# A second fixed order for the mixer: outputs in halves, the next unit's decays ahead, tokens normalized a unit earlier

## The chip, the cores and the metric

The kernel runs on one core of a Trainium2 chip. The metric is the device time of one execution in microseconds (us), and a version is judged by the median of several. The engines are called by the names of the profile: PE (matmuls and transposes), DVE (vector), ACT (scalar, with its function tables), POOL (GpSimd) and SP (issues the DMAs). Everything is float32.

## The reference

The input is 8 images of 32 x 32 positions with 128 channels, treated as 8 batches of T = 1024 tokens with C = 128 channels.

```python
x = x + conv_attention(group_norm(x))            # 4 heads of 32, q and k with unit length
t = to_tokens(x)
t = t + mamba(layer_norm(t), fwd) + reverse(mamba(reverse(layer_norm(t)), bwd))
t = t + stu(layer_norm(t))                       # spectral filters, by FFT
```

The change lies in the second line, the mixer, and at the end of attention. For one batch and one direction:

```python
z, xbc, dt = split(x @ in_proj)                  # 256, 256 + 64 + 64, 4
xh, Bm, Cm = split(silu(causal_conv(xbc, 4)))    # 4 heads of 64; state size 64
dt = softplus(dt + dt_bias); dA = dt * -exp(A_log)
# in 16 chunks of 64 tokens:
Y_diag = C B^T * L * (x dt)                      # L = exp(segment sums of dA), inside a chunk
states = B^T (decay_to_end * x dt)               # one state a chunk
new    = state + carry * chunk_decay             # passed on from chunk to chunk
Y_off  = C carry * decay_from_start
y  = (Y_diag + Y_off + D x) * silu(z)
out = rms_norm(y) @ out_proj
```

## The kernel before

Four stages follow each other. The **setup** loads X, normalizes it, makes q, k and v, and begins the tables of the last stage. **Attention** runs over 128 units (batch b, half of the queries, block j of 128 keys), one in 2.75 us; eight units make one half of a batch. The **mixer** runs over 16 units (batch b, direction d). The **last stage** (layer norm, filters by transforms, sum) begins when the last sum of the mixer has been stored.

*Order.* Work that the text leaves to the framework's scheduler is placed by it. Within `manual_schedule(engines=IN_ORDER)` PE, DVE, ACT and POOL issue exactly in the order of the text. Attention and the mixer's loop stand in such a region; the preparation of the mixer's first unit (from `normalize(0, ...)` to `activate_bc(first)`) does not.

*Attention.* In step n, `scores` computes score products `pt` (L486) on PE into a pool of three buffers, and ACT takes their exponential `pr` (L491). `weigh` multiplies `pr` of step n - 1 with v on PE (`po`, L506) and adds pairs of `pr` on DVE (`two`, L515); `total` sums these over keys with a matmul (`pd`, L526). At the end of a half, `project` takes the reciprocal of the denominators in pieces over the following steps, keeps their extremes in `most` and `least`, multiplies (`av`, L546), projects on PE (`py`, L550) and adds onto X (L554).

Meanwhile POOL mixes the filter weights of the last stage (`mixed`, L231 and L233, and `both`, L245). That text stands ahead of attention's, in the setup. Each part comes by a DMA on SP's queue and is scaled and added.

*Mixer.* The inputs of a unit are made during the unit before it. `normalize` takes mean and variance of a batch's tokens (`b_st`, `b_mv`, DVE) and, through `rsqrt`, the factor `ln_r` on POOL (L117, L119); `normalized` makes `b_shift` (DVE, L651) and the tokens `b_x` (ACT, eight instructions, L654). `turn_tokens` transposes them (`px`) and copies them to `bxt`. `steps` makes the step sizes (`pd`, L685, then small DVE operations and two ACT operations) and `da`. `spread` makes `dau`, 128 x 2048, on POOL (L717). `project_x` and `convolve` make `xs` (projection `pp` on PE, copy `xp` on ACT, three DVE operations for each half, L756), `project_z` the gate `zs`, `project_bc` and `activate_bc` `bt` and `ct`.

In the unit itself, in this order:
- `decays`: three small matmuls into the PSUM tile `misc` (L801), and their exponentials `rest` (L803) and `dec` (L807) on ACT.
- `turn_x`: transposes of `xs` (`sx`, L817) and the product `xdt` (DVE, L820, twice).
- `turn_sums` of the unit before: two transposes in the same `misc` (L1022), `rms_v` (DVE, L1024), `rms` (POOL, L1026).
- `turn_b`: `sb` (PE, L834), its halves go to `bk` (ACT, L842) and `gm` (DVE, L854).
- `decayed_x`: `xdd` (DVE, L849, twice), then `gm`.
- `add_up` of the unit before: eight sums from `spo` onto X (DVE, L1033); with d = 1 X is then stored.
- `between`: `pl` (PE, L863), `lm` = exponential (ACT, L870).
- `chunk_states` and `pass_states`: `pst` (PE, L900), then the chain of states on DVE (L914, L917, 29 instructions), half of which a DMA moves to the other partitions (`moved`).
- `from_start`: `pe` (PE, L880), `ec` = exponential (ACT, L887).
- `weigh_decays`: `lm` times `gm` (L938, twice) and `ec` times `ct` (L942, twice, 128 x 1024 each) on DVE.
- `outputs`: 240 small matmuls `sy` (L966) for all 16 chunks, into two PSUM tiles.
- `gate`: `y` (DVE, L981, L989) and its squares `sq` (ACT, L990).
- `project_out`: `spo` (PE, L996); `square_sums`: `misc` (L1008) and the copy `sums` (ACT, L1016).

The wide PSUM tiles come in two pools of two buffers each: `ps_w` (`px`, `pd`, `pp`, `pz`, `pb`, `sx`, `sb`, `pl`, `pe`) and `ps_s` (`misc`, `pst`, `sy`, `spo`). `bxt`, `dau` and the tokens have one buffer each.

Of the kernel before, what the change touches and what calls it, by code (L numbers as in the profile page):

```python
# [44 lines left out]
def fast_kernel(ctx: ExitStack, tc: tile.TileContext, a: dict, out: bass.AP, bad: bass.AP):  # L45
# [7 lines left out]
    tables_pool = middle.enter_context(tc.tile_pool(name="tables_pool", bufs=1, side="right"))  # L53
    early = ctx.enter_context(ExitStack())
# [3 lines left out]
    def ctile(shape, name):  # L58
        pool = const if name in LASTING else tables_pool if name in ("fwd", "m_u") else passing
        return pool.tile(shape, F32, tag=name, name=name)  # L60
# [314 lines left out]

    with ExitStack() as s:
        keepq = s.enter_context(tc.tile_pool(name="a_q", bufs=1))
        qs, ks, vs = [], [], []  # L380
        with ExitStack() as s2:
# [79 lines left out]
            load_ssm_weights(p1)  # L461

        p1 = s.enter_context(tc.tile_pool(name="a_1", bufs=1))
# [5 lines left out]


        most = p1.tile([P, 2 * B], F32, name="most")
        least = p1.tile([P, 2 * B], F32, name="least")
# [61 lines left out]
        def project(b, half, av, pd):  # L534

            den = p1.tile([P, 512], F32, tag="den", name=f"den{b}_{half}")
            nc.vector.tensor_copy(den, pd)
            yield
            for i in range(4):
                cols = slice(i * P, (i + 1) * P)  # L540
                nc.vector.reciprocal(den[:, cols], den[:, cols])
                if i % 2:
                    yield
            nc.vector.tensor_reduce(most[:, 2 * b + half : 2 * b + half + 1], den, AX.X, ALU.max)
            nc.vector.tensor_reduce(least[:, 2 * b + half : 2 * b + half + 1], den, AX.X, ALU.min)
            nc.vector.tensor_tensor(av, av, den, ALU.mult)  # L546
            yield
            py = ps_t.tile([P, 4, C], F32, tag="t", name=f"py{b}_{half}")
            for i in range(4):
                nc.tensor.matmul(  # L550
                    py[:, i, :], lhsT=av[:, i * P : (i + 1) * P], rhs=wout, start=True, stop=True
                )
            to = X[b][:, half * 4 : half * 4 + 4, :]
            nc.vector.tensor_tensor(to, to, py, ALU.add)  # L554
# [4 lines left out]
        for n in range(len(units) + 2):  # L559
            if n < len(units):  # L560
                prs[n] = scores(*units[n])
            if 2 <= n and units[n - 2][2] % 2:
                b, half, j = units[n - 2]
                total(b, half)
                if j == NT - 1:
                    ending = project(b, half, sums.pop("av"), sums["d"])
            if 1 <= n < len(units) + 1:
                b, half, j = units[n - 1]
                weigh(b, half, j, prs.pop(n - 1))
                if j == NT - 1:  # L570
                    av = p1.tile([P, 512], F32, tag="av", name=f"av{b}_{half}")
                    nc.vector.tensor_copy(av, sums["o"])
                    sums["av"] = av
            next(ending, None)
        for _ in ending:
            pass


        far = ctile([P, 4], "far")
        nc.vector.tensor_reduce(far[:, 0:1], most, AX.X, ALU.max)  # L580
        nc.vector.tensor_reduce(far[:, 1:2], least, AX.X, ALU.min)
        nc.vector.tensor_scalar(far[:, 2:3], far[:, 0:1], 1e25, None, ALU.is_gt)
        nc.vector.tensor_scalar(far[:, 3:4], far[:, 1:2], 1e-30, None, ALU.is_lt)
        pf = ps_o.tile([1, 2], F32, tag="d", name="pf")
        nc.tensor.matmul(pf, lhsT=ones[:, 0:1], rhs=far[:, 2:4], start=True, stop=True)
        nc.vector.tensor_reduce(far[0:1, 0:1], pf, AX.X, ALU.add)
        nc.vector.tensor_copy(bad, far[0:1, 0:1])

    def layer_norm(pool, b, name):
        st = pool.tile([P, NT, 6], F32, tag="ln_st", name=f"{name}_st{b}")  # L590
        mv = pool.tile([P, NT, 2], F32, tag="ln_mv", name=f"{name}_mv{b}")
        for j in range(NT):
            nc.vector.bn_stats(st[:, j, :], X[b][:, j, :])
        for j in range(NT):
            nc.vector.bn_aggr(mv[:, j, :], st[:, j, :])
        rstd = rsqrt(pool, mv[:, :, 1], NT, 1.0, 1e-5, "ln_r")
        xn = pool.tile([P, NT, C], F32, tag="ln_x", name=f"{name}_x{b}")
        for j in range(NT):
            nc.vector.tensor_scalar(
                xn[:, j, :], X[b][:, j, :], mv[:, j, 0:1], rstd[:, j : j + 1], ALU.subtract, ALU.mult  # L600
            )
        return xn
# [7 lines left out]
    with ExitStack() as s:  # L610
# [27 lines left out]
        def normalize(b, seq):  # L638
            st = p1.tile([P, NT, 6], F32, tag="ln_st", name=f"b_st{b}")
            mv = p1.tile([P, NT, 2], F32, tag="ln_mv", name=f"b_mv{b}")  # L640
            for j in range(NT):
                nc.vector.bn_stats(st[:, j, :], X[b][:, j, :])
            for j in range(NT):
                nc.vector.bn_aggr(mv[:, j, :], st[:, j, :])
            rstd = rsqrt(p1, mv[:, :, 1], NT, 1.0, 1e-5, "ln_r")
            seq["mv"], seq["rstd"] = mv, rstd

        def normalized(b, seq):
            mv, rstd = seq["mv"], seq["rstd"]
            shift = p1.tile([P, NT], F32, tag="ln_s", name=f"b_shift{b}")  # L650
            nc.vector.scalar_tensor_tensor(shift, mv[:, :, 0], -1.0, rstd, ALU.mult, ALU.mult)  # L651
            xn = p1.tile([P, NT, C], F32, tag="ln_x", name=f"b_x{b}")
            for j in range(NT):
                nc.scalar.activation(  # L654
                    xn[:, j, :], X[b][:, j, :], AF.Identity, bias=shift[:, j : j + 1], scale=rstd[:, j : j + 1]
                )
            seq["xn"] = xn

        def turn_tokens(b, seq):
            xn = seq["xn"]  # L660
# [3 lines left out]
            xt = p1.tile([P, T + 2 * pad], F32, tag="xt", name=f"bxt{b}")  # L664
# [5 lines left out]
        def steps(b, seq):  # L670
# [27 lines left out]
            yield  # L698
            u = small("sp_u")
            nc.vector.tensor_scalar(u, e, 1.0, None, ALU.add)  # L700
            lg = small("sp_l")
# [11 lines left out]
        def spread(u):  # L713

            u.dt, u.da = u.seq["dt"][:, :, u.heads], u.seq["da"][:, :, u.heads]
            u.dau = p1.tile([P, NT, NH, L], F32, tag="dau", name=f"dau{u.tag}")
# [46 lines left out]
        def project_z(u):  # L763
            u.zs = p2.tile([P, 2, T], F32, tag="zs", name=f"zs{u.tag}")
            for n in range(2):
                pz = projected(u, slice(n * P, (n + 1) * P), f"pz{u.tag}_{n}")
                nc.scalar.activation(u.zs[:, n, :], pz, AF.Silu)  # L767
# [29 lines left out]
        def decays(u, misc):  # L797

            pd = misc[:, 768 : 768 + 3 * NT * NH].rearrange("p (i j h) -> p i j h", i=3, j=NT)
# [45 lines left out]
        def decayed_x(u):  # L845
            u.xdd = p1.tile([P, NT, NH, HP], F32, tag="xdd", name=f"xdd{u.tag}")
            for i in range(2):
# [3 lines left out]
                )  # L851

            u.gm = p1.tile([P, NT, L], F32, tag="gm", name=f"gm{u.tag}")
            nc.vector.tensor_tensor(u.gm, u.pg, upto[u.d].unsqueeze(1).to_broadcast([P, NT, L]), ALU.mult)  # L854
# [80 lines left out]
        def weigh_decays(u):  # L935
            for i in range(2):
                js = slice(4 * i, 4 * i + 4)
                nc.vector.tensor_tensor(  # L938
                    u.lm[:, js], u.lm[:, js], u.gm[:, js].unsqueeze(2).to_broadcast([P, 4, NH, L]), ALU.mult
                )  # L940
            for r in range(2):
                nc.vector.tensor_tensor(  # L942
                    u.ec[:, r], u.ec[:, r], u.ct.unsqueeze(2).to_broadcast([P, NT, 2, L]), ALU.mult
                )

        def outputs(u):

            u.py = [
                wide_psum(ps_s, f"sy{u.tag}_{c}").rearrange("p (n j l) -> p n j l", n=2, j=NT) for c in range(2)
            ]  # L950
            before = {at: k for k, at in enumerate(u.chunks[1:])}
            for j in range(NT) if u.d == 0 else reversed(range(NT)):
# [92 lines left out]
        normalize(0, seqs[0])  # L1045
        normalized(0, seqs[0])
        turn_tokens(0, seqs[0])
        for _ in steps(0, seqs[0]):
            pass
        first = units[0]  # L1050
        spread(first)
        project_x(first)
        project_z(first)
        project_bc(first)
        for n in range(2):
            convolve(first, n)
            activate_x(first, n)
        activate_bc(first)

        s.enter_context(tc.manual_schedule(engines=IN_ORDER))  # L1060
        last = None
        misc = wide_psum(ps_s, "misc")
        for at, u in enumerate(units):
            following = units[at + 1] if at + 1 < len(units) else None
            fresh = following and following.d == 0
            decays(u, misc)
            turn_x(u)
            if last:
                turn_sums(last, misc)
            turn_b(u)  # L1070
            decayed_x(u)
            if last:
                add_up(last)
            if fresh:
                turn_tokens(following.b, following.seq)
            between(u)
            going = iter(())
            if fresh:
                going = steps(following.b, following.seq)
                next(going)  # L1080
            chunk_states(u)
            pass_states(u)
            from_start(u)
            next(going, None)
            if following:
                project_x(following)
                next(going, None)
                spread(following)
                project_z(following)
            weigh_decays(u)  # L1090
            outputs(u)
            if following:
                convolve(following, 0)
                activate_x(following, 0)
                project_bc(following)
# [6 lines left out]
            if u.d == 0 and u.b + 1 < B:  # L1102
                normalize(u.b + 1, seqs[u.b + 1])
# [3 lines left out]
            if u.d == 0 and u.b + 1 < B:  # L1107
                normalized(u.b + 1, seqs[u.b + 1])
# [1080 lines left out]
```

## Time and profile before

| | us |
|---|---|
| median of 3 runs | 1711.31 |
| lowest, highest | 1708.39, 1714.41 |
| the profiled execution's own time | 1705.17 |
| its span in the profile | 1703.5 |
| attention | about 130 to 478.7 |
| first unit's preparation, to its first state | 478.7 to 530.67 |
| mixer from its first state to its end | 530.67 to 1241 |
| last stage | 1241 to the end |
| mean granted clock of PE | 0.949 |

| engine | busy us of the span | share |
|---|---|---|
| PE | 1497.4 | 88% |
| DVE | 1181.0 | 69% |
| ACT | 874.4 | 51% |
| POOL | 446.4 | 26% |

The shares are means over stages that differ, so the stages are read one by one. Lines such as L938 are those of the kernel before. In a group of instructions, "out<-in" gives the program's names; "idle before, <-releaser" is the time that the engine stood just before them and what ended it. A "stretch" is a part of the span with the busy time of each engine in it.

### The profile page before, as it was taken

Reading aid. Unit: us, or ns where it says so; the run is one execution under the profiler, and the core shown is the slowest. Engines: PE = TensorE matmul, PEld = TensorE weight load, DVE = VectorE, ACT = ScalarE, POOL = GpSimd, SP = SyncE. Lnnn points to the kernel's source line nnn. Section 1 sums busy time; section 2 is a strip of 40 time slices with the busy share of each in tenths; the row PEclk is TensorE's granted clock in tenths of the full one; section 3 lists DMA queues with packets and bytes.
Section 4 is the critical chain, followed back from the end, with each engine's and each line's share of the span. In section 5 each row is a group of like instructions: output and inputs, shape, how many; then the busy total and the mean of one; then the engine's idle time right before and its main releaser. Section 6 shows DMA issues by size and latency. Waiting matters only on the chain. (4 is left out here: it accounts for less than half of the span.)

```text
span 1703.5 us, 45615 instructions
## 1 busy us (share of the span) xinstructions
PE 1497.4 (88%) x20118; PEld 926.3 (54%) x20118; DVE 1181.0 (69%) x2211; ACT 874.4 (51%) x1198; POOL 446.4 (26%) x504
## 2 busy tenths in 40 slices
PE   4679999999979898988888889989757999999977
PEld 3432333332335565565555555555546888888862
DVE  6757778777756787877777787778544366677644
ACT  2337776677746555454555555555253255555530
POOL 6428999300010212112111111111045410100100
PEclk9899999999979899999999999989878999999998
DMA  5001212000000000000000000000046722322238
GB/s 143 0 11 55 59 60 63 22 2 1 1 1 13 13 26 13 26 11 23 7 25 13 13 26 13 26 13 26 13 149 211 199 60 60 79 67 72 69 93 315
DMA packets 131958, 89.03 MB, mean 52 GB/s; under 512 B 41480, under 2 KB 114824, under 8 KB 131752
## 3 DMA queue, kind: packets, MB, share of 16 engines
q1 hardware_dynamic: 129640, 81.84, 17.1%
q8 instruction: 160, 2.62, 0.7%
q10 hardware_dynamic: 2112, 4.19, 0.6%
q14 instruction: 46, 0.38, 0.1%
HBM read 44.60 MB, written 33.55 MB: 46 GB/s over the span
## 5 line engine op out<-in xcount | busy, mean ns | idle before, releaser
L491 ACT ACTIVATE pr<-pt 128x1024 f32<-128x1024 f32 x256 | 248.1, 1021 | 101.8 <-PE pt L486 96.9
L1268 DVE COPY gs<-pg 128x512 f32<-128x512 f32 x256 | 164.8, 686 | 84.4 <-PE pg L1257 79.6
L1270 ACT COPY gs<-pg 128x512 f32<-128x512 f32 x256 | 138.8, 595 | 145.9 <-PE pg L1257 130.3
L515 DVE TENSOR_TENSOR two<-pr,pr 128x1024 f32<-128x1024 f32 x128 | 158.3, 1277 | 28.0 <-PE pd L526 28.0
L486 PE MATMUL pt<-q,k 32*128 32x512 f32 x1024 | 162.8, 643 | 4.8 <-DVE taps L362 3.5
L1257 PE MATMUL pg<-taps,mst 32*128 32x128 f32 x4096 | 160.3, 287 | 6.5 <-ACT gs L1270 6.5
L1257 PEld LDWEIGHTS pg<-taps,mst 32*128 32x128 f32 x4096 | 135.9, 189 | 31.3 <-issue 16.7
L1291 PE MATMUL py<-gs,u 128*32 128x128 f32 (+1 forms) x4096 | 144.8, 282 | 0.4 <-ACT gs L1270 0.4
L506 PE MATMUL po<-pr,v 128*32 128x512 f32 x1024 | 136.7, 602 | 0.0
L756 DVE SCALAR_TENSOR_TENSOR xs<-xp,cw,xs 128x1024 f32<-128x1024 f32 x96 | 123.9, 1293 | 4.6 <-ACT xs L748 2.4
L1291 PEld LDWEIGHTS py<-gs,u 128*32 128x32 f32 (+1 forms) x4096 | 112.5, 143 | 15.5 <-ACT gs L1270 0.6
L717 POOL TENSOR_TENSOR dau<-upto,da 128x2048 f32<-128x2048 f32 x16 | 63.8, 3989 | 202.3 <-DVE da L709 125.6
L776 PE MATMUL pb<-bxt,wbc 128*128 128x512 f32 x256 | 114.2, 598 | 0.7 <-ACT zs L767 0.7
L1026 POOL TENSOR_TENSOR rms<-rms_v,mhalf 128x8 f32<-128x8 f32 x16 | 39.3, 2457 | 279.3 <-DVE rms_v L1024 279.3
L486 PEld LDWEIGHTS pt<-q,k 32*128 32x128 f32 x1024 | 55.3, 184 | 102.9 <-PE pt L486 40.2
L966 PE MATMUL sy<-lm,xdt 64*64 64x64 f32 x2048 | 81.7, 247 | 22.2 <-DVE lm L938 19.7
L966 PEld LDWEIGHTS sy<-lm,xdt 64*64 64x64 f32 x2048 | 74.8, 155 | 36.9 <-DVE lm L938 20.6
L1280 POOL TENSOR_SCALAR u<-u 128x512 f32<-128x512 f32 x16 | 23.8, 1490 | 248.0 <-DMA u<-ud 248.0
L917 DVE SCALAR_TENSOR_TENSOR state<-state,dec,pst 128x64 f32<-128x64 f32 x448 | 87.3, 275 | 1.1
L776 PEld LDWEIGHTS pb<-bxt,wbc 128*128 128x128 f32 x256 | 47.2, 189 | 55.6 <-issue 53.8
L966 PE MATMUL sy<-ec,state 64*64 64x64 f32 x960 | 64.2, 245 | 14.0 <-DVE ec L942 11.3
L506 PEld LDWEIGHTS po<-pr,v 128*32 128x32 f32 x1024 | 27.3, 109 | 87.7 <-issue 87.4
(278 smaller groups left out, 2938.5 us busy)
## 6 DMA issues: line engine op xcount, KB each, us to landing
ud<-sp SPq DMA_DIRECT2D x8, 1024.0 KB
u<-ud SPq DMA_DIRECT2D x32, 256.0 KB
yd<-sums SPq DMA_DIRECT2D x32, 256.0 KB
moved<-state SPq DMA_DIRECT2D x48, 128.0 KB
yt<-yd SPq DMA_DIRECT2D x6, 1024.0 KB
X<-in_x SPq DMA_DIRECT2D x8, 512.0 KB
part_p<-in_L_ffn_M_phi_plus SPq DMA_DIRECT2D x32, 128.0 KB
part_m<-in_L_ffn_M_phi_minus SPq DMA_DIRECT2D x32, 128.0 KB
```

Of the source, the lines that this page charges most:

```text
L486: nc.tensor.matmul(pt[:, i, :], lhsT=k[rows, j * P : (j + 1) * P], rhs=q[rows, cols], start=True, stop=True)
L491: nc.scalar.activation(pr[:, 2 * g : 2 * g + 2, :].rearrange("p i t -> p (i t)"), pt.rearrange("p i t -> p (i t)"), AF.Exp,)
L506: nc.tensor.matmul(po[rows, :], lhsT=vs[b][:, j, rows], rhs=pr[:, h, :], start=(j == 0), stop=(j == NT - 1))
L515: nc.vector.tensor_tensor(two, sums["pr"][:, 2 * g : 2 * g + 2, :], pr[:, 2 * g : 2 * g + 2, :], ALU.add)
L756: nc.vector.scalar_tensor_tensor(acc, xp[:, at : at + T], cw[u.d][:, n, i : i + 1], acc, ALU.mult, ALU.add)
L776: nc.tensor.matmul(u.pb[:, i * 512 : (i + 1) * 512], lhsT=wbc[u.d][:, k, :], rhs=xt[:, at : at + 512], start=(k == 0), stop=(k == KC - 1),)
L917: nc.vector.scalar_tensor_tensor(u.state[:, k, h, :], u.state[:, k - 1, h, :], u.dec[:, c, j, h : h + 1], u.pst[c][:, j, h, :], ALU.mult, ...
L966: nc.tensor.matmul(u.py[c][h * HP : (h + 1) * HP, r, j, :], lhsT=left, rhs=right, start=(kind == 0), stop=(kind == 1 or k is None),)
L1257: nc.tensor.matmul(pts[g][:, e, :], lhsT=mst[rows, n * 4 + e, :], rhs=taps[rows, cols].rearrange("p f q m i -> p (f q m i)"), start=True, ...
L1268: nc.vector.tensor_copy(to, frm)
L1270: nc.scalar.copy(to, frm)
L1291: nc.tensor.matmul(py[t * 32 : t * 32 + 32 - 16 * m, q, :], lhsT=u[:, i, m:, :, :, q * FC + f].rearrange("p k b i -> p (k b i)"), rhs=mats ...
```

## The change

All of it is order, buffers and the split of two operations; what is computed stays the same, and the number of PE instructions changes by one.

1. **The mixer's loop.** `turn_x` and `turn_sums` of the unit before now stand ahead of `decays`; the decays use other columns of `misc`. `gm` moves between the two halves of `xdd`. `turn_tokens` of the next batch and `between` stand ahead of `add_up`. `spread` of the next unit stands right behind `chunk_states`, ahead of the chain of states, instead of behind `project_x`. `dau` and `bxt` get two buffers.
2. **Outputs in halves.** `weigh_decays` and `outputs` run in two halves of eight chunks, in the direction of the unit: half 0, its outputs, then half 1. `ec` times `ct` thus becomes four instructions of 128 x 512 for two of 128 x 1024. `project_z` is split: its first half stands ahead of the first outputs, its second behind `convolve` of half 0.
3. **Tokens a unit earlier.** A batch is turned, and its steps are made, in the unit with d = 0 of the batch before, instead of in its unit with d = 1; its normalization begins one unit before that, and `normalized` follows in the unit with d = 1.
4. **The first unit.** Its preparation is written out in the order by hand, behind attention. Batch 0 is normalized inside attention: `normalize(bridge, 0)` at step n = 40 and `normalized(0, ...)` at n = 44 (both halves of X[0] are done by step 22). The projection of the last half of attention, the comparison of the denominators and the normalization of batch 1 stand behind the first unit's preparation.
5. **Memory.** A pool `bridge` holds `av`, `most`, `least` and the normalized tokens over both stages; some constants move to a pool that is closed before attention.

The core of the diff:

```diff
@@ attention
-        def project(b, half, av, pd):
+        def weighted(b, half, av, pd):
...
+            if (b, half) != (B - 1, 1):
+                project(b, half, av, ps_t.tile([P, 4, C], F32, tag="t", name=f"py{b}_{half}"))
...
             next(ending, None)
+            if n == 40:
+                early_norm = normalize(bridge, 0)
+            if n == 44:
+                xns[0] = normalized(0, bridge, *early_norm)
@@ parts of the mixer
-            xt = p1.tile([P, T + 2 * pad], F32, tag="xt", name=f"bxt{b}")
+            xt = p2.tile([P, T + 2 * pad], F32, tag="xt", name=f"bxt{b}")
...
-            u.dau = p1.tile([P, NT, NH, L], F32, tag="dau", name=f"dau{u.tag}")
+            u.dau = p2.tile([P, NT, NH, L], F32, tag="dau", name=f"dau{u.tag}")
...
-            pd = misc[:, 768 : 768 + 3 * NT * NH].rearrange("p (i j h) -> p i j h", i=3, j=NT)
+            pd = misc[:, 256 : 256 + 3 * NT * NH].rearrange("p (i j h) -> p i j h", i=3, j=NT)
...
-        def weigh_decays(u):
-            for i in range(2):
-                js = slice(4 * i, 4 * i + 4)
-                nc.vector.tensor_tensor(
-                    u.lm[:, js], u.lm[:, js], u.gm[:, js].unsqueeze(2).to_broadcast([P, 4, NH, L]), ALU.mult
-                )
+        def weigh_decays(u, half):
+
+            i = half ^ u.d
+            js = slice(4 * i, 4 * i + 4)
+            nc.vector.tensor_tensor(
+                u.lm[:, js], u.lm[:, js], u.gm[:, js].unsqueeze(2).to_broadcast([P, 4, NH, L]), ALU.mult
+            )
             for r in range(2):
                 nc.vector.tensor_tensor(
-                    u.ec[:, r], u.ec[:, r], u.ct.unsqueeze(2).to_broadcast([P, NT, 2, L]), ALU.mult
-                )
+                    u.ec[:, r, js], u.ec[:, r, js], u.ct[:, js].unsqueeze(2).to_broadcast([P, 4, 2, L]), ALU.mult
+                )
@@ the first unit, and the loop
-        normalize(0, seqs[0])
-        normalized(0, seqs[0])
-        turn_tokens(0, seqs[0])
...
+        s.enter_context(tc.manual_schedule(engines=IN_ORDER))
+        first, norms = units[0], {}
+        turn_tokens(0, seqs[0])
+        project_x(first)
+        going = steps(0, seqs[0])
+        next(going)
+        project_z(first, 0)
+        next(going)
+        next(going, None)
+        spread(first)
+        convolve(first, 0)
+        project_z(first, 1)
+        project_bc(first)
+        activate_x(first, 0)
+        convolve(first, 1)
+        activate_bc(first)
+        activate_x(first, 1)
+        project(B - 1, 1, av, wide_psum(ps_w, "last_py")[:, :512].rearrange("p (i c) -> p i c", i=4))
+        compare_denominators(most, least, wide_psum(ps_w, "pf")[0:1, :2])
+        xns[1] = normalized(1, bridge, *normalize(bridge, 1))
...
-            fresh = following and following.d == 0
-            decays(u, misc)
+
+            going, fresh = iter(()), u.b + 1 if u.d == 0 and u.b + 1 < B else 0
             turn_x(u)
             if last:
                 turn_sums(last, misc)
+            decays(u, misc)
             turn_b(u)
             decayed_x(u)
+            if fresh:
+                turn_tokens(fresh, seqs[fresh])
+            between(u)
             if last:
                 add_up(last)
             if fresh:
-                turn_tokens(following.b, following.seq)
-            between(u)
-            going = iter(())
-            if fresh:
-                going = steps(following.b, following.seq)
+                going = steps(fresh, seqs[fresh])
                 next(going)
+            if u.d == 1 and u.b + 2 < B:
+                xns[u.b + 2] = normalized(u.b + 2, bridge, *norms.pop(u.b + 2))
             chunk_states(u)
+            if following:
+                spread(following)
             pass_states(u)
             from_start(u)
             next(going, None)
             if following:
                 project_x(following)
-                next(going, None)
-                spread(following)
-                project_z(following)
-            weigh_decays(u)
-            outputs(u)
+            weigh_decays(u, 0)
+            next(going, None)
+            if following:
+                project_z(following, 0)
+            outputs(u, 0)
+            weigh_decays(u, 1)
             if following:
                 convolve(following, 0)
+                project_z(following, 1)
                 activate_x(following, 0)
+            outputs(u, 1)
```

## The prediction

> **What bounds the kernel now.** I read the split by stage first, since the page's share of busy time (PE 88%) mixes stages with different limits. Columns: stretch in us, its length, busy us of each engine, granted clock.
>
> ```profile
> 130.00:478.70 348.70, 348.68 (x2656) 105.70 (x2656) 264.40 (x284) 244.24 (x252) 172.39 (x156) 1.00 0.11 32
> 478.70:530.67 51.97, 38.26 (x226) 23.57 (x228) 24.89 (x51) 28.19 (x36) 5.84 (x7) 0.74 0.00 1
> 530.67:1208.24 677.57, 603.10 (x7730) 389.92 (x7728) 519.00 (x1060) 360.34 (x459) 112.34 (x86) 0.96 0.07 18
> 1208.24:1241.00 32.76, 17.38 (x314) 13.83 (x310) 17.78 (x48) 4.53 (x5) 1.63 (x1) 0.77 0.06 16
> ```
>
> Attention (first line) has PE busy throughout: whatever stops PE there is paid in full. The mixer, from its first chunk's states at 530.67 to its end at 1241, has PE idle 74 us in the third line and a clock below 1. The last stage waits for all of the mixer and isn't changed. Next, the waits of PE over six pairs of units (612.59 to 1159.05, 91.1 us a pair): total us, times, longest.
>
> ```profile
> PE misc L1022 <- ACT dec L807: 21.6, 6, 3.8
> PE sy L966 <- DVE lm L938: 12.7, 6, 2.1
> PE sy L966 <- DVE ec L942: 12.2, 18, 0.8
> PE misc L801 <- ACT sums L1016: 5.9, 12, 0.5
> PE pl L863 <- DVE gm L854: 1.9, 4, 0.5
> ```
>
> With 5.2 of "issue" and 1.4 of small ones this is 60.9 us, 10.15 a pair. Why lm is late, the groups of the same stretch say:
>
> ```profile
> L938 DVE TENSOR_TENSOR lm<-lm,gm 128x1024 f32<-128x1024 f32 x24 | 57.2, 2423 | 0.0
> L942 DVE TENSOR_TENSOR ec<-ec,ct 128x1024 f32<-128x1024 f32 x24 | 28.2, 1212 | 0.0
> ```
>
> The columns after the bar are busy us, mean ns of one, idle before. Same form, same size, twice the time: the timeline has POOL's dau running beside each slow one. Last, what attention holds where the change puts the first batch's normalization. Two stretches of 22 us (one half of a batch's queries), POOL's busy time ahead of the clock:
>
> ```profile
> 251.10:273.10 22.00, 22.00 (x172) 6.71 (x174) 17.38 (x19) 15.51 (x16) 20.40 (x18) 1.00 0.20 60
> 317.10:339.10 22.00, 22.00 (x172) 6.71 (x172) 16.29 (x19) 15.51 (x16) 0.04 (x1) 1.00 0.04 13
> ```
>
> The same two operations on POOL between 229 and 317, then the timeline of DVE at the place and of POOL at the end of its mixing (start, duration):
>
> ```profile
> L231 POOL TENSOR_SCALAR part_m<-part_m,w 128x256 f32<-128x256 f32 x12 | 27.1, 2260 | 4.0 <-DMA part_m<-in_L_ffn_M_phi_minus 4.0
> L231 POOL TENSOR_SCALAR part_p<-part_p,w 128x256 f32<-128x256 f32 x12 | 11.1, 924 | 0.9 <-DMA part_p<-in_L_ffn_M_phi_plus 0.9
> ```
> ```profile
> 248.51 0.96 DVE L546 TENSOR_TENSOR av<-av,den 128x512 f32<-128x512 f32 x1
> 251.02 0.69 DVE L554 TENSOR_TENSOR X<-X,py 128x512 f32<-128x512 f32 x1 [1.54 <-PE py L550]
> ```
> ```profile
> 315.11 2.03 POOL L245 TENSOR_TENSOR both<-plus,minus 128x128 f32<-128x128 f32 x4
> 477.10 0.31 POOL L618 MEMSET chunk_rows<- 128x256 f32 x1 [159.95 <-PE po L506]
> ```
>
> POOL mixes filter weights without a break until 317.1, one group in 22.0 us, then rests for 160 us. Of two equal operations in it, part_p takes 0.92 and part_m 2.26.
>
> **What the Trainium skill says.** "SBUF — State Buffer", section "SBUF: two separate sides": the port pair that DVE and GpSimd share is an exclusive lock for the whole instruction, and a DVE operation with two SBUF inputs takes it against a GpSimd one. The trace agrees: lm 1.21 alone, up to 4.64 beside dau; part_m 0.92 or 2.5, when DVE's `two` (two inputs) runs. "Perfetto Trace Analysis", section "Tensor Engine Instruction (MATMUL, LD_WEIGHTS)": ACT, DVE and GPSIMD are strict FIFO; so one waiting instruction holds all behind it. "TensorE: Matmul & The Clock Gate", section "What's actually happening": half clock after an idle window of about 3.4 us. The trace agrees: after the 3.6 us wait for dec the two halves of sb take 1.97 and 1.86, elsewhere 1.15 and 1.10; with the slower sy, about 2.7 us a pair.
>
> **1. The first normalization within attention: +58.** The built program's order puts ln_r of batch 0 on POOL behind the last `both`, since all mixing comes earlier in the text. At n=44 b_shift follows on DVE behind the av product (ends 249.5 above), and eight b_x on ACT ahead of exponential 44; both engines run in order. b_shift waits for ln_r, so DVE and ACT stand, and PE, which ran pt(46) at 250.91, has no free score buffer. When does POOL finish? At 251.1 three groups are left. A group is 8 scalings at 0.92, 6 additions at 0.73 and 4 `both` at 0.51: 13.8 us, plus 0.08 between instructions and 1 to 2 of waits for part DMAs, about 16.5 when DVE no longer takes the port. So 251.1 + 3 × 16.5 = 300.6; ln_r 0.2 + 1.65; b_shift 0.2; b_x 8 in 3.2; one exponential 1.0, and 0.4 between these: PE goes on at 307.3, 56.4 late, and about 1.7 of cold clock. **58.** Ends: DMA without a wait, 14.5 a group, +52; POOL no faster than now, +75. No cover exists: PE is 100% busy here and nothing later in attention has slack. Of the step's own work (bn 2.3 on DVE, 3.2 on ACT) nothing counts; both have 5 us in 22 idle.
>
> **2. The first unit's start: +2.** Projections come under the order by hand. The copy of bxt needs memory that the last av product (484.8) still uses, so little begins earlier; ahead of the first xdt now stand the last projection's four matmuls (1.2), its sum on X (0.7), seven small comparisons on DVE, and normalization 1 (bn 2.3, ACT 3.2). I get the first states at 532.5 against 530.67; bounds 526 and 535.
>
> **3. The mixer's order: −38.** PE's steps in a unit, start to start: decays 0.67, sx 1.78, sums turned 0.38, sb 2.0, pl 3.5, pst 1.9, pe 3.55, pp 3.55, pz 3.5, sy 4.3, pb 6.97, spo 3.67, squares 1.07: 36.84; where the next batch is turned (px 1.09, pd 1.78), 39.71. Now a pair is 76.55 + 10.15 idle + 2.7 cold + 1.7 of stretched steps.
> Gone: misc<-dec (3.6 a pair) with its cold clock, since squares are turned ahead of the decays; lm against dau, since dau moves up to POOL's place right after rms; sy<-ec and sy<-lm (4.1), since the first half of the outputs has its operands while half the products are left.
> New, walked from t=0 at sx. DVE: xdt twice, then rms_v at 3.55 (misc is one tile, so PE's decays wait for rms_v): decays 3.6, PE idle 1.4. sb 4.3 to 6.3, pl to 9.75. ACT: table load behind decays' release (1.28), rest 5.0. DVE: xdd0 5.15 to 6.35, gm behind bk 7.05 to 7.7, then xdd1. POOL: rms until 6.25, then dau 3.62 until 9.9: xdd1, two inputs, waits for it and ends at 10.9. Then X's eight sums, 2.15: 13.05. pst, in the buffer of the former spo, waits for these: PE idle 3.3 and about 1.35 of cold clock. With d=0, px and pd (2.87) lie in that gap and leave 0.45. ec in halves: 4 instructions for 2, some +0.3 of DVE, hidden by the first outputs. Normalization a unit ahead: 2.0 (b_shift<-ln_r) is already off PE's path now. Queues: SP's order of DMAs is unchanged.
> So d=0: 39.71 + 1.4 + 0.45 + 0.3 (pl<-gm) + 0.6 (issue) = 42.45; d=1: 36.84 + 1.4 + 3.3 + 1.35 + 0.3 = 43.2; a pair 85.65, 5.5 less. From 532.5: the rest of unit 0 27.3, 7 × 43.2, 6 × 42.45, unit 14 (no px) 43.2, unit 15 to its states 13.05: 1173.2. Then the tail, 31.5 (now 32.7; no dau in either): 1204.7 for 1240.8, **−36** with step 2's +2 in it. Ends: −15 (pair 89: cold clock in both units, halves that bring new stalls) and −65 (pair 81).
>
> **Sum:** +58 − 36 = +22 on the profiled execution's own 1705.2 (span 1703.5): 1727. The median of the runs shown is 6 above that execution: **1733**.
>
> **Rivals.** *Faster: the order frees PE more than the stall costs.* If xdd1 gets the port before dau, it ends at 8.9, the sums at 11.05, pst idles 1.3 and nothing goes cold: d=1 39.8, d=0 42.0, a pair 81.8, 9.3 less, some 60 in all; with the short stall (52) −8: 1703. It decides from 9 us a pair (58 over 6.5 pairs). For: rms and xdd0 end within 0.1 us of each other. Against: gm stands between, waiting for bk, while dau's operands are ready. *Much slower: POOL doesn't speed up,* +75, as the mixing may hang on its DMAs (idle 0.4 to 0.6 ahead of each part_m now); with −36 to −15, +39 to +60: 1750 to 1771. *The change doesn't do what it says:* if ln_r got ahead of the mixing there is no stall: −36, 1675. Against: the order in the built program.
>
> **How the numbers follow.** Main case 0.63 (1715 to 1750), much slower 0.17, faster by the mixer 0.14 (a third of it within what can't be told from no change), no stall 0.06. A measurement of this kernel tells 0.3%, 5 us, from no change. Faster 0.15, same 0.08, slower 0.77; range 1703 to 1762.
>
> **What would show it.** Right: DVE idle some 50 us in one piece, "<-POOL ln_r", between 250 and 305, ACT and PE with it, POOL's part_m at 0.92 in it; decays waiting for DVE rms_v, pst for DVE X; xdd with a maximum of 3 us or more; lm at 1.2; units of both directions 42 to 44 us. Wrong: no gap in attention; a pair above 89 or below 82; first states more than 6 us from 532.5 plus the stall.

## The result, and the profile after

| | before | after |
|---|---|---|
| median of 4 runs each (one more before than in the first table), us | 1710.26 | 1729.7 |
| lowest, highest | 1708.39, 1714.41 | 1727.82, 1733.67 |
| span of the profiled execution | 1703.5 | 1728.8 |

The ratio is 1.0113, with a 95% interval from 1.0087 to 1.014: slower by 19.4 us, 1.1%, which is clear of the noise. The forecast was 1733, with 22 more.

By stage, the changed kernel (stretch, length, busy us of PE, of its weight loads PEld, of DVE, ACT and POOL, granted clock, DMA): attention from its first copy of `av` to its last, the first unit to its first state, the mixer from state to state, and its tail.

```profile
152.26:540.30 388.04, 331.89 (x2516) 101.02 (x2516) 250.90 (x287) 234.70 (x248) 135.28 (x144) 0.93 0.09 26
540.30:595.25 54.95, 40.32 (x256) 25.87 (x256) 28.70 (x57) 25.18 (x35) 10.78 (x14) 0.78 0.00 1
595.25:1232.63 637.38, 594.58 (x7706) 381.79 (x7704) 504.60 (x1069) 357.36 (x449) 99.48 (x81) 0.97 0.08 19
1232.63:1264.90 32.27, 17.91 (x314) 14.42 (x310) 17.92 (x50) 4.53 (x5) 1.64 (x1) 0.84 0.07 16
```

PE no longer fills attention: 332 busy of 388. Before, the same two copies lie at 147.87 and 477.49, 329.62 apart. Set beside the prediction's steps (tail: to the issue of the last store of X, 1264.5, before 1240.8):

| stage | before | after | change | forecast |
|---|---|---|---|---|
| attention | 329.6 | 388.0 | +58.4 | +58 |
| first unit, last `av` to first state | 53.2 | 54.95 | +1.8 | +2 |
| first state to last unit's first state | 677.6 | 637.4 | −40.2 | −36.9 |
| tail | 32.6 | 31.9 | −0.7 | −1.2 |
| sum | | | +19.3 | +22 |

The two profiled executions differ by 25.3, because the setup was 4.4 longer and the last stage 1.6. Neither is put down to the change: over all profiles of this study the first copy of `av` lies between 147.9 and 154.2, and in nine of them the last stage takes 461.5 to 464.3, with no pattern by kernel.

The gap itself, in the timelines of DVE, ACT, PE and POOL (start, duration, idle before and what ended it):

```profile
252.91 0.97 DVE L596 TENSOR_TENSOR av<-av,den 128x512 f32<-128x512 f32 x1
307.10 0.17 DVE L415 SCALAR_TENSOR_TENSOR b_shift<-b_mv,ln_r 128x8 f32<-128x8 f32 x1 [53.21 <-POOL ln_r L128]
```
```profile
307.30 3.18 ACT L418 ACTIVATE b_x<-X,b_shift,ln_r 128x128 f32<-128x128 f32 x8 [55.21 <-DVE b_shift L415]
```
```profile
311.44 2.98 PE L536 MATMUL pt<-q,k 32*128 32x512 f32 x8 [56.15 <-ACT pr L541]
```
```profile
255.54 0.92 POOL L240 TENSOR_SCALAR plus<-part_p,w 128x256 f32<-128x256 f32 x1
256.44 0.92 POOL L240 TENSOR_SCALAR minus<-part_m,w 128x256 f32<-128x256 f32 x1
...
272.08 0.92 POOL L240 TENSOR_SCALAR plus<-part_p,w 128x256 f32<-128x256 f32 x1
...
303.33 1.68 POOL L254 TENSOR_TENSOR both<-plus,minus 128x128 f32<-128x128 f32 x4
305.10 0.20 POOL L126 TENSOR_SCALAR ln_r_v<-b_mv 128x8 f32<-128x8 f32 x1
305.39 1.67 POOL L128 TENSOR_TENSOR ln_r<-ln_r_v,mhalf 128x8 f32<-128x8 f32 x1
```

The chain reads backwards: PE waits for an exponential, ACT's exponentials stand behind `b_x`, `b_x` waits for `b_shift`, that for `ln_r`, and `ln_r` comes on POOL directly behind the last `both`. With DVE silent, a group of the mixing takes 16.5 us (255.54 to 272.08) for 22.0, and `part_m` 0.92 for 2.26 in the mean.

In the mixer the waits of PE before have gone and others stand in their place (total us, times, longest; whole execution), and the operation that is held beside `dau` is now `xdd`, no longer `lm` (groups, 636.8 to 1193; the last line is `xdd` in the kernel before, 580 to 1180):

```profile
PE misc L802 <- DVE rms_v L1029: 21.4, 15, 1.4
PE pst L902 <- DVE X L1038: 11.9, 9, 1.6
PE pl L865 <- DVE gm L856: 5.0, 5, 3.3
PE pst L902 <- DVE xdd L850: 4.4, 5, 0.9
PE sy L971 <- DVE lm L941: 3.7, 1, 3.7
```
```profile
L718 POOL TENSOR_TENSOR dau<-upto,da 128x2048 f32<-128x2048 f32 x13 | 58.3, 4488 | 0.0
L850 DVE TENSOR_TENSOR xdd<-xdt,rest 128x1024 f32<-128x1024 f32 x26 | 52.8, 2032 | 21.1 <-ACT rest L804 21.1
L941 DVE TENSOR_TENSOR lm<-lm,gm 128x1024 f32<-128x1024 f32 x26 | 31.7, 1219 | 0.0
L1031 POOL TENSOR_TENSOR rms<-rms_v,mhalf 128x8 f32<-128x8 f32 x13 | 21.3, 1638 | 297.2 <-DVE rms_v L1029 297.2
```
```profile
L849 DVE TENSOR_TENSOR xdd<-xdt,rest 128x1024 f32<-128x1024 f32 x26 | 30.6, 1219 | 0.0
```

In the mean `lm` is at 1.22 (2.42 before) and `xdd` at 2.03 (1.22 before). DVE idles 21.1 us for `rest`, the exponential of the decays that now come later.

### The profile page after: what moved, and what is told of

Its sections match the earlier page's. It is cut to its first block, busy times and chain, and to the rows that moved or that the text cites. A ratio compares the mean times of both kernels' runs of the same rounds, so it can differ in the third digit from the quotient of the medians.

```text
span 1728.8 us, 45643 instructions
## 1 busy us (share of the span) xinstructions
PE 1499.5 (87%) x20118; PEld 926.6 (54%) x20118; DVE 1168.9 (68%) x2243; ACT 871.7 (50%) x1195; POOL 419.9 (24%) x504
## 5 line engine op out<-in xcount | busy, mean ns | idle before, releaser
L1307 PEld LDWEIGHTS py<-gs,u 128*32 128x32 f32 (+1 forms) x4096 | 112.5, 143 | 15.5 <-ACT gs L1286 0.6
L1031 POOL TENSOR_TENSOR rms<-rms_v,mhalf 128x8 f32<-128x8 f32 x16 | 26.2, 1637 | 369.6 <-DVE rms_v L1029 369.6
L850 DVE TENSOR_TENSOR xdd<-xdt,rest 128x1024 f32<-128x1024 f32 x32 | 60.6, 1895 | 26.8 <-ACT rest L804 26.8
L718 POOL TENSOR_TENSOR dau<-upto,da 128x2048 f32<-128x2048 f32 x16 | 71.2, 4450 | 16.2 <-DVE da L710 16.2
L971 PEld LDWEIGHTS sy<-lm,xdt 64*64 64x64 f32 x2048 | 58.3, 136 | 27.7 <-issue 12.5
L576 PE MATMUL pd<-two,ones 128*32 128x512 f32 x512 | 69.6, 604 | 0.0
```

The source lines that it names most:

```text
L718: nc.gpsimd.tensor_tensor(u.dau, upto[u.d].unsqueeze(1).unsqueeze(1).to_broadcast([P, NT, NH, L]), u.da.unsqueeze(3).to_broadcast([P, NT, ...
L1307: nc.tensor.matmul(py[t * 32 : t * 32 + 32 - 16 * m, q, :], lhsT=u[:, i, m:, :, :, q * FC + f].rearrange("p k b i -> p (k b i)"), rhs=mats ...
```

## The experiments

The first series moves the suspected gap, and adds it alone; then each of the two new waits of the mixer is taken away; then parts of the change are undone; last, what gained is put together. Ratios are to the kernel before in the same series (medians 1710.1 to 1712.3), with 95% intervals. Differences below are between medians; across series they are good to some 3 us.

| kernel | median us | ratio |
|---|---|---|
| late | 1676.42 | 0.980 [0.9778, 0.9821] |
| insert_only | 1769.14 | 1.0331 [1.0314, 1.0349] |
| late_sums_mid | 1655.98 | 0.9673 [0.9657, 0.9689] |
| late_dau_behind | 1657.51 | 0.9682 [0.9665, 0.9698] |
| late_whole | 1679.32 | 0.9818 [0.9802, 0.9835] |
| late_oldhead | 1631.98 | 0.9543 [0.9522, 0.9563] |
| late_dau_old | 1660.66 | 0.9712 [0.9696, 0.9729] |
| late_both | 1629.92 | 0.9534 [0.9518, 0.955] |
| tokens_only | 1646.96 | 0.9611 [0.9591, 0.963] |
| best1 | 1616.47 | 0.9439 [0.9414, 0.9463] |
| best2 | 1623.07 | 0.9476 [0.9458, 0.9495] |

**late.** The gap's place in attention.

```diff
-            if n == 40:
+            if n == 88:
                 early_norm = normalize(bridge, 0)
-            if n == 44:
+            if n == 92:
                 xns[0] = normalized(0, bridge, *early_norm)
```

> The changed kernel with the normalization of batch 0 at steps 88 and 92 of attention in place of 40 and 44, some 50 us after POOL has ended its mixing; nothing else differs. Theory (the gap is the wait for POOL's mixing, and nothing but that): attention's gap of 56.2 us goes with its cold clock, b_shift waits under 3 us, 1730 - 58 = 1672, which is 38 below the kernel before. Rival (the eight b_x and the statistics ahead of the exponentials cost on their own, wherever they stand): a gap of 4 to 6 us stays, 1676 to 1680. Rival (the mixer's gain hangs on the late start, since weights or tables of the last stage are otherwise in the way): above 1690.

1676.4, 53 below the changed kernel (1729.7). The gap is gone, though not all of it. The half of a batch that holds the insertion takes 28.4 us (copies of `av` at 370.18 and 398.59) for 22.0. ACT's and PE's timelines of it:

```profile
383.21 3.18 ACT L418 ACTIVATE b_x<-X,b_shift,ln_r 128x128 f32<-128x128 f32 x8 [1.61 <-DVE b_shift L415]
```
```profile
387.35 2.98 PE L536 MATMUL pt<-q,k 32*128 32x512 f32 x8 [2.55 <-ACT pr L541]
390.26 1.94 PE L556 MATMUL po<-pr,v 128*32 128x512 f32 x8
392.13 2.09 PE L536 MATMUL pt<-q,k 32*128 32x512 f32 x8
394.15 1.45 PE L576 MATMUL pd<-two,ones 128*32 128x512 f32 x8
395.42 1.03 PE L556 MATMUL po<-pr,v 128*32 128x512 f32 x8
```

ACT stands 1.61 us for `b_shift`, which comes behind a product of `av` on DVE, and then runs the eight `b_x` in one piece. This stops PE for 2.55 us. Then eight pt take 2.98 us for 1.14 to 1.37, and PE is slow until about 395; this costs another 3.9. So of the 58.4, some 52 are the wait for POOL's mixing and 6.4 the step's own work: the first rival, with 4 to 6 us that stay, was right, and the theory too low.

**insert_only.** The kernel before, and in its attention:

```diff
             next(ending, None)
+            if n == 40:
+                ...                      # bn_stats, bn_aggr on X[0]; e_r = rsqrt(...)
+            if n == 44:
+                ...                      # e_shift on DVE; 8 ACT instructions into one small tile
```

> The kernel before with only the inserted work: statistics and ln_r of batch 0 at step 40 of attention, b_shift and eight ACT instructions like b_x at step 44, into a small tile that nobody reads (the mixer normalizes batch 0 again as before). Theory (the gap is POOL's order alone): b_shift waits for ln_r some 53 us, attention is 58 longer, 1710 + 58 = 1768. Rival (the gap needs the new memory layout or the hand order of the mixer): within 5 us of 1710.

1769.1: 57 above the kernel before of its series, for 58; in its profile attention takes 389.6 for 329.6. The order on POOL alone makes the gap; neither the memory layout nor the mixer is needed:

```profile
304.06 0.17 DVE L585 SCALAR_TENSOR_TENSOR e_shift<-e_mv,e_r 128x8 f32<-128x8 f32 x1 [52.97 <-POOL e_r L119]
```

**late_sums_mid.** From late; `turn_x` takes the halves that it is to do.

```diff
-            turn_x(u)
+            turn_x(u, (0,))
             if last:
                 turn_sums(last, misc)
+            turn_x(u, (1,))
             decays(u, misc)
```

> As late, with turn_sums between the two halves of turn_x, so that rms_v stands ahead of the second xdt on DVE and the decays need not wait for it 1.4 us a unit. Theory (this wait is on the path of every unit with a unit before it, because rest, xdd, X and pst hang on the decays): 1.2 us in each of 15 units, 18 in all, 1654 if late is 1672. Rival (what is won there is lost again behind dau's hold of the port, xdd still ending when dau lets go, and pst waits longer): 0 to 5, 1667 to 1672.

20.4 less than late, for 18. PE's wait for rms_v falls from 21.4 to 4.5 us in all and DVE's for `rest` from 26.8 to 9.8. The rival's mechanism is there as well: `xdd` grows from 1.83 to 2.13 us in the mean, and pst's wait for X from 10.4 to 14.7; yet it takes back only a part.

**late_dau_behind.** From late, with one element of `xdd` copied by POOL ahead of `dau`.

```diff
             if following:
+                nc.gpsimd.tensor_copy(hold, u.xdd[:, NT - 1, NH - 1, HP - 1 : HP])
                 spread(following)
```

(In the run the copy stands inside `spread`, which is given the unit.)

> As late, with one tiny POOL copy ahead of dau that reads the last element of the second xdd half, so that dau begins only when xdd is done and falls beside X's sums and the chain of states (which have one SBUF input besides PSUM). Theory (dau's lock is what makes the second xdd 1.7 to 3.2 us and pst late): the second xdd takes 1.2, pst waits under 0.7, rms stays 1.64; 0.5 to 1.5 us in each unit, 8 to 22 in all, 1650 to 1664 if late is 1672. Rival (dau now collides with lm again): lm above 2 us, no gain or slower, 1672 to 1690. Rival (the sums of X are held by dau too): X's eight at over 3 us, within 4 of late.

18.9 less than late. Groups of the whole execution:

```profile
L722 POOL TENSOR_TENSOR dau<-upto,da 128x2048 f32<-128x2048 f32 x16 | 58.9, 3682 | 16.2 <-DVE da L710 16.2
L854 DVE TENSOR_TENSOR xdd<-xdt,rest 128x1024 f32<-128x1024 f32 x32 | 39.0, 1220 | 26.8 <-ACT rest L808 26.8
```

`xdd` is at 1.22 for 1.83 in late, `dau` at 3.68 for 4.45, `lm` still at 1.22, X's eight sums take 2.15, and pst's longest wait is 0.6. Neither rival held.

**late_whole.** From late, with both halves of the products, then of the outputs, undivided in place.

```diff
-            weigh_decays(u, 0)
             next(going, None)
             if following:
                 project_z(following, 0)
+                project_z(following, 1)
+            weigh_decays(u, 0)
+            weigh_decays(u, 1)
             outputs(u, 0)
-            weigh_decays(u, 1)
+            outputs(u, 1)
             if following:
                 convolve(following, 0)
-                project_z(following, 1)
                 activate_x(following, 0)
-            outputs(u, 1)
```

> As late, with the outputs undivided again: both halves of weigh_decays, after both halves of project_z, ahead of all outputs, and convolve of half 0 behind them (the four instructions for ec stay). Theory (with dau away from lm, PE's 10.6 us of pe, pp and pz behind pst cover the states and most of the products, so halves are worth at most half a us a unit): 1676 + 0 to 10. Rival (the waits of the outputs, 36 us in the kernel before, went because of the halves): they come back, 1700 to 1712.

2.9 more than late, with overlapping intervals: with this order of the head the halves are worth a few us at most, and perhaps nothing.

**late_oldhead.** From late, with the decays first again.

```diff
+            decays(u, misc)
             turn_x(u)
             if last:
                 turn_sums(last, misc)
-            decays(u, misc)
```

> As late, with the decays ahead of turn_x again, as in the kernel before; so PE's turned sums wait for the exponentials dec, and rest comes some 3 us earlier than in late. Theory (dec was late in the kernel before only because ACT stood at b_x ahead of it, which is now elsewhere; the wait is then under 1.5 us, no more than the 1.4 for rms_v that it replaces, and xdd begins earlier): 1660 to 1676. Rival (dec takes table load and three exponentials, and the 3.8 us come back in every second unit with a cold clock): 1690 to 1705.

44.4 less than late, more than twice what its theory gave at best. One line for the mixer, then groups on POOL and DVE (577.8 to 1096), PE's waits at the head of a unit (whole execution), and ACT's timeline there:

```profile
539.01:1134.71 595.70, 575.18 (x7706) 364.30 (x7704) 489.90 (x1070) 355.96 (x449) 109.55 (x81) 1.00 0.08 20
```
```profile
L1031 POOL TENSOR_TENSOR rms<-rms_v,mhalf 128x8 f32<-128x8 f32 x13 | 32.6, 2509 | 272.5 <-DVE rms_v L1029 272.5
L850 DVE TENSOR_TENSOR xdd<-xdt,rest 128x1024 f32<-128x1024 f32 x26 | 31.6, 1215 | 0.0
```
```profile
PE misc L802 <- ACT sums L1021: 7.4, 15, 0.5
PE pst L902 <- DVE X L1038: 5.5, 9, 0.6
PE sb L835 <- DVE xdt L821: 4.5, 16, 1.1
```
```profile
965.33 0.37 ACT L1021 COPY sums<-misc 128x256 f32<-128x256 f32 x1 [0.75 <-PE misc L1013]
965.72 1.28 ACT L804 ACT_TABLE_LOAD   x1
967.01 0.20 ACT L804 ACTIVATE rest<-misc 128x32 f32<-128x32 f32 x1
967.10 0.38 ACT L808 ACTIVATE dec<-misc 64x32 f32<-64x32 f32 x2
```

The same place in the kernel before, where the next batch's tokens still stand between:

```profile
1105.33 0.37 ACT L1016 COPY sums<-misc 128x256 f32<-128x256 f32 x1 [0.75 <-PE misc L1008]
1107.05 3.18 ACT L654 ACTIVATE b_x<-X,b_shift,ln_r 128x128 f32<-128x128 f32 x8 [1.35 <-DVE b_shift L651]
1110.24 1.28 ACT L803 ACT_TABLE_LOAD   x1
1111.53 0.20 ACT L803 ACTIVATE rest<-misc 128x32 f32<-128x32 f32 x1
```

PE's turned sums don't wait for dec at all: it is ready 2.2 us after the copy `sums` began; with `b_x` between it was 6.7. `rest` is there when `xdt` ends, so `xdd` runs at once, and `rms` on POOL (2.51, held by `xdd`; 1.64 in the changed kernel) keeps `dau` behind it. In the loop the longest of these waits is 0.6 (the 1.1 is in the first unit), the granted clock is 1.00 for 0.97, and PE is busy 575 us for the same work that takes 595 in the changed kernel. So putting the decays behind the turned sums cost 44 us, with both of its consequences: the wait itself, and `xdd` late enough to fall into `dau`; late_both takes away these two alone and comes to the same time.

**late_dau_old.** From late, `dau` in one buffer, spread behind `project_x`.

```diff
-            u.dau = p2.tile([P, NT, NH, L], F32, tag="dau", name=f"dau{u.tag}")
+            u.dau = p1.tile([P, NT, NH, L], F32, tag="dau", name=f"dau{u.tag}")
...
-                spread(following)
             pass_states(u)
...
                 project_x(following)
+                spread(following)
```

> As late, with dau in one buffer and its spread behind project_x, as in the kernel before, so that it waits for pe's matmuls and falls beside lm and ec. Theory (dau's place decides who is held: xdd is free, pst no longer waits, but lm is at 3 to 4 us a half and the outputs wait): what xdd wins, about 19 us as with dau behind xdd, is lost again and more, 1676 to 1700. Rival (the halves give PE enough to do while lm is held): 1657 to 1665.

15.8 less than late; the rival held. `lm` is held again, though only to 2.65 us at most (4.64 before), and PE has the gate's projection and the first half of the outputs meanwhile. Beside this head, `dau`'s new place was a loss of 16 us.

**late_both.** The edits of late_sums_mid and late_dau_behind together.

> Both edits that gained: turn_sums between the halves of turn_x, and dau behind the second xdd. Each alone took 19 to 20 us off late. Theory (two different waits in a row on one path, rms_v ahead of the decays and xdd ahead of pst, so they add): 1637. Rival (both shorten the same DVE chain and PE becomes the bound after the first): 1648 to 1656.

46.5 less than late, where the single gains add to 39.3: they add, and a little more.

**tokens_only.** late_oldhead with the edits of late_whole and late_dau_old as well (spread behind `project_x` and the step sizes of the fresh batch).

> As late_oldhead, with the outputs undivided and dau in one buffer behind project_x too: of the mixer's change there remain the tokens that are normalized and turned a unit earlier, gm between the halves of xdd, between ahead of add_up, and the first unit by hand. Theory (what the mixer gains comes from b_x and the turned tokens, which leave the decays' exponentials and the fresh unit's head free; halves are worth 3, dau's place next to nothing once xdd isn't behind it): 1635 to 1645. Rival (dau's move away from lm carries a good part, since the outputs waited 36 us for lm and ec): 1655 to 1680.

15 more than late_oldhead by the medians, 12 by the ratios: 2 above the theory's range and 8 below the rival's, so neither held. Of late_oldhead's 78 us below the kernel before, halves and `dau`'s place together give 12 to 15, with `lm` at a mean of 1.54 without them. The other 65 belong to tokens a unit earlier, `gm` between the halves of `xdd`, and `between` ahead of X's sums, which weren't told apart by runs. The first unit's order is not among the gains: from the last copy of `av` to the first state tokens_only takes 56.5 us, late_oldhead 54.6, the kernel before 53.2.

**best1.** From late_oldhead.

```diff
-            if n == 92:
-                xns[0] = normalized(0, bridge, *early_norm)
+            if n == 90:
+                pieces = normalized_in_pieces(0, bridge, *early_norm)
+                xns[0] = next(pieces)          # b_shift
+            if n > 90:
+                next(pieces, None)             # one b_x
...
         turn_tokens(0, seqs[0])
+        project(B - 1, 1, av, ...)
         project_x(first)
+        compare_denominators(...)
+        norm = normalize(bridge, 1)
...
-        spread(first)
...
         convolve(first, 1)
+        nc.gpsimd.tensor_copy(hold, first.xs[:, 1, T - 1 : T])
+        spread(first)
```

> As late_oldhead, with b_x of batch 0 given to ACT one a step from step 91 on, and in the first unit the last projection, the comparison and the statistics of batch 1 ahead (beside PE's wait for bxt) and dau behind both convolves. Theory (ACT has 0.7 us free in each step of attention, so the 6 us that one half of a batch is longer go; DVE's six convolve operations take 7.8 in place of 11.0 without dau, and xdt doesn't wait 2.8 us for b_shift): 6 + 3 + 3 less than late_oldhead, 1620. Rival (the first unit hangs on PE's own chain, so only attention gains): 1626.

15.5 less than late_oldhead, for 12. Attention is back at 329.6 (copies of `av` from 150.3 to 479.9); from the last of these to the first state 46.5 us pass for 54.6 in late_oldhead. This is 5.6% faster than the kernel before.

**best2.** From best1, with the copy of late_dau_behind in the loop.

> As best1, with dau held behind the second xdd in every unit. Theory (with the decays first, xdd is no longer held by dau, 1.2 us each, so there is nothing left to win): within 4 us of best1. Rival (rms, 2.5 us beside xdd, and pst's 0.6 us for X go with it): 6 to 10 us less.

Nothing is gained. The median is 6.6 above best1's, with intervals that just overlap, so neither the theory (within 4) nor the rival (6 to 10 less) is borne out. In the profiles the mixer, from state to state, takes 597.7 us for 595.7. The decays' order has already done what holding `dau` did, and these figures speak for a small loss by the extra copy.

## Why the prediction was right, and where it was not

**Step 1 (+58, measured +58.4) was right in mechanism and size.** The order in the built program showed the queue on POOL, the page showed how long it lasts, and PE 100% busy in that stage showed that nothing hides it. The estimate of 16.5 us a group rested on POOL's operations being free of DVE's, and measured 16.5. late and insert_only show the mechanism from both sides. One sentence of it failed: "of the step's own work nothing counts; both have 5 us in 22 idle". It costs 6.4 us (late): ACT's idle time lies in pieces of some 0.7 a step, and 1.61 us of waiting with 3.18 of `b_x` in one piece exceed what three score buffers bridge. best1, with `b_shift` two steps earlier and one `b_x` a step, pays nothing for it.

**Step 2 (+2, measured +1.8) was right.** Its bound, memory still in use by attention, shows as POOL's wait of 7.15 us for the last product of `av`, ahead of its writes to `bxt` and `xp`, and PE's of 6.3 behind it.

**Step 3 (−36.9 to the last unit's states, measured −40.2) was right in mechanism: a pair 85.65, measured 85.8** (state to state from 636.83 to 1151.66, six pairs). The wait of the decays for rms_v measured 1.4, as worked out. In the unit that starts at 1050.6 `xdd` ended 10.9 us into it, as worked out, though by another way: `rms` took 1.64, not 2.5, since `xdd` came later than it, and `dau` took 4.6, held by the first `xdd`.

That the pair came out so near is in part luck. The same six pairs in the changed kernel, then in late_oldhead:

```profile
636.83:1151.66 514.83, 479.07 (x6194) 308.55 (x6192) 408.75 (x865) 289.94 (x368) 83.47 (x70) 0.97 0.08 19
```
```profile
577.87:1057.50 479.63, 463.10 (x6195) 294.29 (x6193) 393.93 (x866) 289.90 (x371) 91.50 (x70) 1.00 0.08 21
```

PE stood 6.0 us a pair where the prediction's terms give 7.75: pst waited 0.9 + 1.6 in five of the eight units with d = 1 and about 1 or less in the others, for 3.3 in each. PE was busy 79.8 us a pair for 77.9. At the full clock of late_oldhead (1.00 for 0.97) the same work takes 77.2, so some 2.7 a pair go with the lower clock, where the prediction gave it 1.35. The two errors cancel. The 3.3 us by which the whole stretch was pessimistic lie elsewhere, mainly in the last two steps from state to state: 41.4 and 39.6 for 43.2 each. The last unit has no unit after it and so no `dau` that holds `xdd`; the sum let it be held there too.

**What the sum hid is whose gain it was.** The prediction put the end of misc<-dec down to the reordered sums, and that of sy<-lm and sy<-ec to `dau` and the halves. late_oldhead has the old order and no such wait: before, dec was late because eight `b_x` (3.18 us) stood ahead of it on ACT, and the tokens normalized a unit earlier took these away (the lines of ACT show it; no run moves them alone). The reorder itself cost 44 us. The halves gave a few us or nothing beside it, and with the old head 12 to 15 together with `dau`'s place. A forecast that adds up waits gets the total right where it follows every queue, and can still credit the wrong edit.

**The rivals.** "Faster" put `xdd` ahead of `dau`, with a pair of 81.8, and needed some 82.2. late_dau_behind makes this order, with a pair of 82.5 (six pairs, state to state), and took 19 us off late. Set against the gap, that would bring the changed kernel level with the one before, not below it. "Much slower" asked for a POOL that doesn't speed up; it did. "No stall" was excluded by the order.

## What to carry to other kernels

Before a small step is put into another stage, look at the queue of each engine that it crosses: it waits for everything in front of it there, and in-order engines hand the wait on, so one tiny POOL operation behind 50 us of filler work stopped the three others, DVE, ACT and PE. Give inserted work to a saturated stage in pieces that fit the slack of a single step. A reorder that removes one wait should be tried without the edits that go with it: here one of them cost 44 us, more than half of what the others gained.

## What the runs showed of the hardware that was not expected

A gap of 2.55 us on PE was enough to lose the clock (late: eight pt 2.98 for 1.14; the granted clock is 1.00 up to 387.85 and 0.50 from 388.35 to 394.5), where the Trainium skill, "TensorE: Matmul & The Clock Gate", section "What's actually happening", speaks of an idle window of about 3.4 us; here the shorter gap sufficed. All eight profiles with this gap show it (2.84 to 2.98 us). In the changed kernel's mixer 0.9 and 1.6 us, 0.4 apart, did the same: 58 pst in 3.29 us, where 64 take 1.98. Yet in the kernel before one of the waits for dec, 3.06 us long, left the clock at 1.00, and `sb` behind it took 1.15, as without a wait. So the length of a gap alone doesn't decide, and what else does is not shown here.

```profile
1022.07 1.98 PE L902 MATMUL pst<-xdd,bk 64*64 64x128 f32 x64
...
1061.59 0.44 PE L902 MATMUL pst<-xdd,bk 64*64 64x128 f32 x4 [0.89 <-DVE xdd L850]
1063.66 3.29 PE L902 MATMUL pst<-xdd,bk 64*64 64x128 f32 x58 [1.64 <-DVE X L1038]
```
```profile
838.35 0.44 PE L1022 MATMUL misc<-ident,sums 128*128 128x128 f32 x2 [3.06 <-ACT dec L807]
838.71 1.15 PE L834 MATMUL sb<-ident,bt 64*64 64x64 f32 x32
```

DVE also holds the small POOL operation: `rms` on 128 x 8 elements takes 1.64 alone (changed kernel) and 2.51 beside `xdd` (late_oldhead).
